# A two-direction state-space mixer: GpSimd's difference behind a VectorE shift, row scaling ahead of a logarithm, and the last unit's pieces in another order

## The chip, the cores and the metric

The kernel runs on one core of a Trainium2 chip. The core has five engines, each with its own in-order queue of instructions: TensorE (PE; its weight loads are shown as PEld), VectorE (DVE), ScalarE (ACT), GpSimd (POOL) and SyncE (SP), which here issues nearly all DMA transfers. Engines wait for each other through semaphores. The metric is the time of one execution in microseconds (us). Before the change the median of three runs is 1452.74 us (1451.16 to 1455.33).

## The reference

The input is x of shape 8 x 32 x 32 x 128 (8 sequences of 1024 tokens with 128 channels), all float32. Three stages follow each other, each added to a residual.

```python
x = x + conv_attention(group_norm(x))          # 4 heads, full attention per sequence
t = to_tokens(x)                               # (8, 1024, 128)
t = t + mixer_fwd(ln(t)) + reverse(mixer_bwd(reverse(ln(t))))
t = t + spectral_filter(ln(t))                 # 16 filters and 3 taps, one of 4 banks chosen
```

One direction of the mixer does, per sequence:

```python
z, xbc, dt = split(x @ in_proj)
xbc = silu(causal_conv4(xbc))                  # 4 taps along the tokens
xh, B, C = split(xbc)                          # 4 heads of 64 channels; state of 64
dt = softplus(dt + dt_bias); A = -exp(A_log)
# in chunks of 64 tokens: within a chunk exp of differences of cumulated dt*A,
# between chunks a state that decays and is passed on
y  = ssd(xh, dt, A, B, C) + xh * D
yg = y * silu(z)
out = (yg * rsqrt(mean(yg * yg) + eps) * norm_w) @ out_proj
```

## The kernel before

Everything that fits stays in SBUF: X holds the 8 sequences as tiles of 128 tokens x 8 x 128 channels. There are four stages in time: attention (0 to some 465 us), the mixer (465 to 1046), the transforms of the spectral filter (1046 to 1135), and its products and way back (1135 to the end). The order of instructions is written out by hand: inside each stage the program text is the order of each engine's queue (`manual_schedule`), in the mixer also SP's.

The mixer works in 16 units, one per sequence b and direction d (d = 0 forward, d = 1 backward), in the order (0,0), (0,1), (1,0) and so on. The loop body (from L1263) treats unit `u`, prepares `following` (its projections and convolution) and finishes `last` (its output projection). The pieces that matter here:

- `from_row` (L908) on GpSimd: the difference between a row of cumulated decays and a column of them, 128 x 2048 elements, read from SBUF and written in place into `lm`. By a dependency added by hand (`behind`) it waits for one more instruction, so that it runs beside the passing of states. In the loop that instruction is `following.convolved`, the second tap of the following unit's convolution on VectorE (L964). `between` (L918) on ScalarE then clips `lm` (Relu) and later takes its exponential.
- `normalize` and `normalized` prepare the layer norm of a later sequence. `normalize` takes statistics on VectorE (L446, L448) and the power -1/2 on GpSimd (L130, L132, tile `ln_r`). `normalized` then makes the shift -mean * rstd on VectorE (L453, 128 x 8, two SBUF inputs) and applies scale and shift on ScalarE (L458), eight pieces of 128 x 128, in two halves with a `yield` between them. In the loop only backward units call `normalized`.
- `chunk_states` (L1066) on TensorE makes one state per chunk in two PSUM tiles `pst`; `pass_states` on VectorE runs one copy (L1082) and 28 steps (L1085), each reading the state before it from SBUF and `pst` from PSUM. After steps 7 and 14 SP sends the states to the other half of the partitions (`moved`, L1098).
- `project_bc` (L986, tile `pb`) on TensorE follows the chunk states. `outputs(u, 0)` and `outputs(u, 1)` (L1133, tile `sy`) follow it; each is 120 to 128 small matmuls. Their PSUM tiles come from the pool `ps_s` of two buffers, the same ones as `pst`, so they also wait until the states are passed. `turn_x` (L1015, L1018) then starts the next unit.
- `end` runs the output projection of a unit (L1164, tile `spo`), sums of squares (L1176), their turning (L1190, `rms_v` L1192 on VectorE), and the power -1/2 on GpSimd (L1194, `rms`). `scale_rows` (L1202) multiplies the projected rows on ScalarE, reading PSUM; `add_rows` (L1206) adds them to X on VectorE.
- `steps` computes softplus for a fresh sequence, as a generator that is resumed by `next(going)`: matmuls (L491), small VectorE operations, Exp (L505), then u + 1 on VectorE (L508) and the logarithm on ScalarE (L510, with a table load), and last small VectorE operations (L512 to L517). Forward units with a sequence to come run it.

The last unit (7,1) stands outside of the loop. Beside its own work it finishes unit (7,0) and starts the next stage for sequence 0: `turn_spectra` (L528), `block_spectra` as generator `spectra(k)` (matmuls L539 into `pf`, a copy L547 on ScalarE; then L550 on VectorE and L554, L557 on GpSimd), `regress` (L569, tile `pu`), `add_taps` (L579) and `store_residual`. PSUM has 8 banks: `ps_w` (two buffers of two banks) and `ps_s` (the same) in the mixer; `ps_f`, `ps_t` and `ps_o` in the stage after it.

Of the kernel before, what the change touches and what calls it, by code (L numbers as in the profile page):

```python
# [8 lines left out]
F32 = mybir.dt.float32  # L9
# [5 lines left out]
P = 128  # L15
# [15 lines left out]
NB = 2  # L31
# [14 lines left out]
def fast_kernel(ctx: ExitStack, tc: tile.TileContext, a: dict, out: bass.AP, bad: bass.AP):  # L46
# [395 lines left out]
    def normalize(pool, b):  # L442
# [5 lines left out]
            nc.vector.bn_aggr(mv[:, j, :], st[:, j, :])  # L448
        return mv, rsqrt(pool, mv[:, :, 1], NT, 1.0, 1e-5, "ln_r")

    def normalized(b, pool, mv, rstd, wide=None):
        shift = pool.tile([P, NT], F32, tag="ln_s", name=f"b_shift{b}")
        nc.vector.scalar_tensor_tensor(shift, mv[:, :, 0], -1.0, rstd, ALU.mult, ALU.mult)  # L453
        xn = xns[b] = (wide or resid).tile([P, NT, C], F32, tag="ln_x", name=f"ln_x{b}")
        for j in range(NT):
            if j == NT // 2:
                yield
            nc.scalar.activation(  # L458
                xn[:, j, :], X[b][:, j, :], AF.Identity, bias=shift[:, j : j + 1], scale=rstd[:, j : j + 1]
            )  # L460
# [361 lines left out]
    with ExitStack() as s:  # L822
# [18 lines left out]
        def wide_psum(pool, name):  # L841

            return pool.tile([P, 1024], F32, tag="w", name=name)
# [60 lines left out]
        def from_row(u, other):  # L904

            t = nc.gpsimd.tensor_tensor(  # L908
                u.lm, u.cs.unsqueeze(3).to_broadcast([P, NH, NT, L]), u.lm, ALU.subtract
            )  # L910
            if other:
                behind(t, other, "beside the states")
# [158 lines left out]
                            stop=True,  # L1071
                        )

        def pass_states(u, among=range(2 * NT - 1)):

            if 0 in among:
                u.state = p1.tile([P, 2 * NT - 1, 2, HP], F32, tag="state", name=f"state{u.tag}")
                u.moved = p1.tile([P, NT, 2, HP], F32, tag="moved", name=f"moved{u.tag}")
            for k in among:
                j, c = u.chunks[k]  # L1080
                if k == 0:
                    nc.vector.tensor_copy(u.state[:, 0], u.pst[c][:, j])  # L1082
                else:
                    for h in range(2):
                        nc.vector.scalar_tensor_tensor(  # L1085
                            u.state[:, k, h, :],
                            u.state[:, k - 1, h, :],
                            u.dec[:, c, h, j : j + 1],
                            u.pst[c][:, j, h, :],
                            ALU.mult,  # L1090
                            ALU.add,
                        )
                if k in (7, 14):
                    for r in range(2):

                        ks = [m for m in range(0 if k == 7 else 8, k + 1) if u.chunks[m + 1][1] != r]
                        to = slice((1 - r) * L, (2 - r) * L)
                        nc.sync.dma_start(  # L1098
                            u.moved[to, ks[0] // 2 : ks[-1] // 2 + 1],
                            u.state[r * L : (r + 1) * L, ks[0] : ks[-1] + 1 : 2],  # L1100
                        )
# [96 lines left out]
        def scale_rows(u):  # L1198

            u.rows = u.y[:, 0, :].rearrange("p (j c) -> p j c", j=NT)  # L1200
            for j in range(NT):
                nc.scalar.activation(u.rows[:, j, :], u.po[:, j, :], AF.Identity, scale=u.rstd[:, j : j + 1])  # L1202
# [60 lines left out]
        for at, u in enumerate(units[:-1]):  # L1263
# [34 lines left out]
            next(going, None)  # L1298
            next(going, None)
            first_tap(following, 0)  # L1300
            next(going, None)
            if last:
                scale_rows(last)

            b = (u.b + 2) % B
            norm = None
# [5 lines left out]
                project_z(u, n)  # L1312
                activate_z(u, n)
            first_tap(following, 1)
            from_row(following, following.convolved)
            for _ in normalized(b, bridge, *norm) if u.d else ():
                pass
            between(following, AF.Relu, 1.0)
            chunk_states(u)
            pass_states(u)  # L1320
# [35 lines left out]
        gate(last, 1)  # L1356
        ut = tokens.tile([P, T + 2 * pad], F32, tag="xt", name="ut0")[:, : T + 4].rearrange("p (r t) -> p r t", r=4)
        copy_turned(ut, pt)
        pass_states(u, range(8))
        end(last, ps_w)  # L1360
        pass_states(u, range(8, 2 * NT - 1))
        scale_rows(last)
        sp = p2.tile([P, 2, T], F32, tag="xs", name="sp0").rearrange(
            "p a (c k i q f) -> p (a c) k i q f", k=NB, i=2, q=4, f=FC
# [15 lines left out]
            pass  # L1380
        reload(stored)
        outputs(u, 0)
        outputs(u, 1)
        making = spectra(1, "ec")
        next(making)
        add_x(u, "xdd")
        gate(u, 0)
        gate(u, 1)
        po = wide_psum(ps_w, "pu0").rearrange("p (k r c) -> p k r c", k=NB, r=4)
        for k in range(NB):  # L1390
            regress(0, k, ut, po[:, k])
        norming = normalized(1, bridge, *norm)
        next(norming)
        for _ in making:
            pass
        store_spectra(0, sp)
        end(u, ps_s)
        for _ in norming:
            pass
        for k in range(NB):  # L1400
            add_taps(0, k, po[:, k])
        store_residual(0)
# [10 lines left out]
    with ExitStack() as s:  # L1413
# [4 lines left out]
        with ExitStack() as s2:  # L1418
            p1 = s2.enter_context(tc.tile_pool(name="f_1", bufs=1))
            p2 = s2.enter_context(tc.tile_pool(name="f_2", bufs=2))  # L1420
            ps_f = s2.enter_context(tc.tile_pool(name="f_ps_f", bufs=2, space=PSUM))
            ps_t = s2.enter_context(tc.tile_pool(name="f_ps_t", bufs=1, space=PSUM))
            ps_o = s2.enter_context(tc.tile_pool(name="f_ps_o", bufs=2, space=PSUM))

            def turned(n):
# [1012 lines left out]
```

## Time and profile before

| | |
|---|---|
| median of 3 runs | 1452.74 us (1451.16 to 1455.33) |
| the profiled execution | 1452.17 us |
| its span, first to last instruction | 1450.4 us |
| TensorE busy | 1341.4 us (92%) |
| VectorE busy | 1119.2 us (77%) |
| ScalarE busy | 915.4 us (63%) |
| GpSimd busy | 528.1 us (36%) |
| DMA, mean | 85 GB/s |
| granted TensorE clock, mean | 0.980 |

Times in the views are in us from the start of the span, those of groups in ns. `out<-in` are the program's names of tiles. A wait is put down to the instruction that ended it; "issue" means that no such instruction is seen. L numbers are lines of the kernel; where a helper makes the instruction, the line is the helper's.

### The profile page before, as it was taken

What the parts mean: (1) busy time and instruction counts of PE and PEld (TensorE: products, weight loads), DVE (VectorE), ACT (ScalarE), POOL (GpSimd) and SP (SyncE); (2) the same over time, 40 slices, a digit from 0 to 9 for tenths busy, and PEclk for the clock granted to TensorE, in tenths of its full rate; (3) what the DMA queues carried; (4) which work ended last, traced back from release to release, by engine and by line L of the source; (5) the groups of instructions that cost most, each with busy time, mean ns of one, the idle gap of its engine ahead of it and who ended that gap; (6) DMA issues with size and microseconds to landing.
All of it is one profiled execution on the core that took longest, in us unless ns stands there. A gap on an engine that the chain in (4) does not pass through costs nothing. (4 is left out here: it accounts for less than half of the span.)

```text
span 1450.4 us, 45285 instructions
## 1 busy us (share of the span) xinstructions
PE 1341.4 (92%) x19782; PEld 842.2 (58%) x19782; DVE 1119.2 (77%) x2138; ACT 915.4 (63%) x1421; POOL 528.1 (36%) x510
## 2 busy tenths in 40 slices
PE   5999999999998899999989999999789899999977
PEld 2223333233333566666666666666679899999963
DVE  5779889688768598989898989898554677777745
ACT  2666666666756677778777777776344455555520
POOL 3327866875500332334342323233377111111100
PEclk9999999999999999999999999999989999999989
DMA  7101111110002333434333444442368323222258
GB/s 178 41 1 30 45 38 37 37 52 23 8 1 47 82 79 75 103 75 103 89 90 89 91 93 108 96 98 48 99 200 223 97 70 91 73 76 69 72 149 320
DMA packets 139382, 123.09 MB, mean 85 GB/s; under 512 B 44808, under 2 KB 118152, under 8 KB 135080
## 3 DMA queue, kind: packets, MB, share of 16 engines
q1 hardware_dynamic: 137064, 115.93, 31.1%
q10 hardware_dynamic: 2112, 4.19, 0.8%
q8 instruction: 157, 2.57, 0.7%
q14 instruction: 49, 0.40, 0.1%
HBM read 78.15 MB, written 34.08 MB: 77 GB/s over the span
## 5 line engine op out<-in xcount | busy, mean ns | idle before, releaser
L692 ACT ACTIVATE pr<-pt 128x1024 f32<-128x1024 f32 x256 | 248.1, 1021 | 117.2 <-PE pt L687 115.7
L717 DVE TENSOR_TENSOR two<-pr,pr 128x1024 f32<-128x1024 f32 x128 | 163.4, 1317 | 21.4 <-ACT pr L692 20.5
L1512 ACT COPY gs<-pg 128x512 f32<-128x512 f32 x256 | 132.7, 602 | 64.2 <-PE pg L1499 47.8
L1510 DVE COPY gs<-pg 128x512 f32<-128x512 f32 x256 | 158.7, 682 | 15.1 <-PE pg L1499 9.7
L687 PE MATMUL pt<-q,k 32*128 32x512 f32 x1024 | 160.1, 653 | 7.0 <-ACT pr L692 4.7
L1499 PE MATMUL pg<-taps,mst 32*128 32x128 f32 x4096 | 145.9, 282 | 4.7 <-ACT gs L1512 3.8
L1499 PEld LDWEIGHTS pg<-taps,mst 32*128 32x128 f32 x4096 | 134.1, 190 | 16.7 <-issue 11.4
L922 POOL TENSOR_TENSOR ec<-ec,ct 128x2048 f32<-128x2048 f32 x16 | 83.4, 5212 | 163.9 <-ACT cums L864 143.0
L708 PE MATMUL po<-pr,v 128*32 128x512 f32 x1024 | 141.7, 609 | 0.0
L1533 PE MATMUL py<-gs,u 128*32 128x128 f32 (+1 forms) x4096 | 128.2, 277 | 0.2 <-DVE gs L1510 0.2
L964 DVE SCALAR_TENSOR_TENSOR xs<-xp,cw,xs 128x1024 f32<-128x1024 f32 x96 | 121.8, 1282 | 3.5 <-issue 1.7
L986 PE MATMUL pb<-bxt,wbc 128*128 128x512 f32 x256 | 115.7, 605 | 8.6 <-ACT zs L977 6.0
L1533 PEld LDWEIGHTS py<-gs,u 128*32 128x32 f32 (+1 forms) x4096 | 112.2, 141 | 7.7 <-DVE gs L1510 0.4
L1522 POOL TENSOR_SCALAR u<-u 128x512 f32<-128x512 f32 x16 | 23.9, 1497 | 229.2 <-PE pg L1499 157.6
L687 PEld LDWEIGHTS pt<-q,k 32*128 32x128 f32 x1024 | 47.3, 186 | 86.2 <-issue 30.3
L1085 DVE SCALAR_TENSOR_TENSOR state<-state,dec,pst 128x64 f32<-128x64 f32 x448 | 87.4, 274 | 1.1
L986 PEld LDWEIGHTS pb<-bxt,wbc 128*128 128x128 f32 x256 | 47.7, 192 | 67.1 <-issue 54.9
L1133 PE MATMUL sy<-lm,xdt 64*64 64x64 f32 x2048 | 68.3, 224 | 17.5 <-DVE state L1085 10.5
L1194 POOL TENSOR_TENSOR rms<-rms_v,mhalf 128x8 f32<-128x8 f32 x16 | 26.2, 1636 | 151.3 <-DVE rms_v L1192 151.3
L708 PEld LDWEIGHTS po<-pr,v 128*32 128x32 f32 x1024 | 27.7, 110 | 89.5 <-issue 85.3
L1133 PEld LDWEIGHTS sy<-lm,xdt 64*64 64x64 f32 x2048 | 61.3, 136 | 30.8 <-issue 28.1
L908 POOL TENSOR_TENSOR lm<-cs,lm 128x2048 f32<-128x2048 f32 x16 | 57.9, 3617 | 46.6 <-DVE xs L964 19.5
(280 smaller groups left out, 2808.3 us busy)
## 6 DMA issues: line engine op xcount, KB each, us to landing
lm<-cd SPq DMA_DIRECT2D x32, 512.0 KB
ec<-cd SPq DMA_DIRECT2D x32, 512.0 KB
ud<-sp SPq DMA_DIRECT2D x8, 1024.0 KB
u<-ud SPq DMA_DIRECT2D x32, 256.0 KB
yd<-sums SPq DMA_DIRECT2D x32, 256.0 KB
moved<-state SPq DMA_DIRECT2D x48, 128.0 KB
yt<-yd SPq DMA_DIRECT2D x6, 1024.0 KB
X<-in_x SPq DMA_DIRECT2D x8, 512.0 KB
```

The lines of the kernel that those rows point to most:

```text
L687: nc.tensor.matmul(pt[:, i, :], lhsT=k[rows, j * P : (j + 1) * P], rhs=q[rows, cols], start=True, stop=True)
L692: nc.scalar.activation(pr[:, 2 * g : 2 * g + 2, :].rearrange("p i t -> p (i t)"), pt.rearrange("p i t -> p (i t)"), AF.Exp, scale=SCALE,)
L708: nc.tensor.matmul(po[rows, :], lhsT=vs[b][:, j, rows], rhs=pr[:, h, :], start=(j == 0), stop=(j == NT - 1))
L717: nc.vector.tensor_tensor(two, sums["pr"][:, 2 * g : 2 * g + 2, :], pr[:, 2 * g : 2 * g + 2, :], ALU.add)
L964: u.convolved = nc.vector.scalar_tensor_tensor(acc, xp[:, at : at + T], cw[u.d][:, n, i : i + 1], acc, ALU.mult, ALU.add)
L986: nc.tensor.matmul(u.pb[:, i * 512 : (i + 1) * 512], lhsT=wbc[u.d][:, k, :], rhs=xt[:, at : at + 512], start=(k == 0), stop=(k == KC - 1),)
L1085: nc.vector.scalar_tensor_tensor(u.state[:, k, h, :], u.state[:, k - 1, h, :], u.dec[:, c, h, j : j + 1], u.pst[c][:, j, h, :], ALU.mult, ...
L1133: nc.tensor.matmul(u.py[c][h * HP : (h + 1) * HP, r, j, :], lhsT=left, rhs=right, start=(kind == 0), stop=(kind == 1 or k is None),)
L1499: nc.tensor.matmul(pts[g][:, e, :], lhsT=mst[rows, n * 4 + e, :], rhs=taps[rows, cols].rearrange("p f q m i -> p (f q m i)"), start=True, ...
L1510: nc.vector.tensor_copy(to, frm)
L1512: nc.scalar.copy(to, frm)
L1533: nc.tensor.matmul(py[t * 32 : t * 32 + 32 - 16 * m, q // 2, :], lhsT=u[:, i, m:, :, :, q * FC + f].rearrange("p k b i -> p (k b i)"), rhs ...
```

## The change

There are four edits.

1. In the loop, `from_row(following, ...)` stands behind `normalized` in the program text, and in backward units it waits for that normalization's shift (kept in the list `shifted`) in place of the convolution's second tap. Forward units wait as before.
2. `scale_rows(last)` stands ahead of the resumption of `steps` that issues u + 1 and the logarithm.
3. In the last unit the states are passed in one go, ahead of `end(last)`; the second block's spectra start between the two halves of the outputs; one half of `regress` and the first half of `normalized` come ahead of `add_x` and the gates; the second half of `normalized` comes ahead of `end(u)`, and the second half of `regress` behind it.
4. In the stage after the mixer, the PSUM pool `ps_t` is opened ahead of `ps_f` and so takes the first two banks.

```diff
+    shifted = []
+
     def normalized(b, pool, mv, rstd, wide=None):
         shift = pool.tile([P, NT], F32, tag="ln_s", name=f"b_shift{b}")
-        nc.vector.scalar_tensor_tensor(shift, mv[:, :, 0], -1.0, rstd, ALU.mult, ALU.mult)
+        shifted.append(
+            nc.vector.scalar_tensor_tensor(shift, mv[:, :, 0], -1.0, rstd, ALU.mult, ALU.mult)
+        )
...
-        def pass_states(u, among=range(2 * NT - 1)):
-
-            if 0 in among:
-                u.state = p1.tile([P, 2 * NT - 1, 2, HP], F32, tag="state", name=f"state{u.tag}")
-                u.moved = p1.tile([P, NT, 2, HP], F32, tag="moved", name=f"moved{u.tag}")
-            for k in among:
-                j, c = u.chunks[k]
+        def pass_states(u):
+
+            u.state = p1.tile([P, 2 * NT - 1, 2, HP], F32, tag="state", name=f"state{u.tag}")
+            u.moved = p1.tile([P, NT, 2, HP], F32, tag="moved", name=f"moved{u.tag}")
+            for k, (j, c) in enumerate(u.chunks[:-1]):
...
             first_tap(following, 0)
-            next(going, None)
             if last:
                 scale_rows(last)
+            next(going, None)
...
             first_tap(following, 1)
-            from_row(following, following.convolved)
             for _ in normalized(b, bridge, *norm) if u.d else ():
                 pass
+            from_row(following, shifted[-1] if u.d else following.convolved)
             between(following, AF.Relu, 1.0)
...
-        pass_states(u, range(8))
+        pass_states(u)
         end(last, ps_w)
-        pass_states(u, range(8, 2 * NT - 1))
         scale_rows(last)
...
         outputs(u, 0)
-        outputs(u, 1)
         making = spectra(1, "ec")
         next(making)
+        outputs(u, 1)
+        po = wide_psum(ps_w, "pu0").rearrange("p (k r c) -> p k r c", k=NB, r=4)
+        regress(0, 0, ut, po[:, 0])
+        norming = normalized(1, bridge, *norm)
+        next(norming)
         add_x(u, "xdd")
         gate(u, 0)
         gate(u, 1)
-        po = wide_psum(ps_w, "pu0").rearrange("p (k r c) -> p k r c", k=NB, r=4)
-        for k in range(NB):
-            regress(0, k, ut, po[:, k])
-        norming = normalized(1, bridge, *norm)
-        next(norming)
+        for _ in norming:
+            pass
         for _ in making:
             pass
         store_spectra(0, sp)
         end(u, ps_s)
-        for _ in norming:
-            pass
+        regress(0, 1, ut, po[:, 1])
         for k in range(NB):
             add_taps(0, k, po[:, k])
...
+            ps_t = s2.enter_context(tc.tile_pool(name="f_ps_t", bufs=1, space=PSUM))
             ps_f = s2.enter_context(tc.tile_pool(name="f_ps_f", bufs=2, space=PSUM))
-            ps_t = s2.enter_context(tc.tile_pool(name="f_ps_t", bufs=1, space=PSUM))
             ps_o = s2.enter_context(tc.tile_pool(name="f_ps_o", bufs=2, space=PSUM))
```

## The prediction

> **What bounds the kernel now.** I read the busy table by stretch first, then the waits of the stretch that the diff touches, then single tiles and the order of time. Between 465 and 1010 us (the mixer's loop over units) TensorE is busy 503.9 of 545.0 us, VectorE 468.0, ScalarE 415.4, GpSimd 194.5: TensorE paces it, and a gain there must close a TensorE gap. The chain that ended last reaches back only to 1044 us, so it says nothing of the loop. The waits in the loop (who waited, for what, us in total, times, longest):
>
> ```profile
> PE sy L1133 <- DVE state L1085: 10.5, 7, 1.5
> PE pst L1066 <- ACT y L1202: 2.8, 6, 0.7
> PE sy L1133 <- issue: 4.7, 5, 1.5
> ACT ln_x L458 <- DVE b_shift L453: 8.3, 7, 1.2
> ```
>
> Seven waits of 1.5 us are one for each backward unit (d = 1) that has a successor; six are one for each forward unit with a fresh sequence. Who is late in the first? The row of the shift's line (152 ns at least, 3577 at most), then the timeline of VectorE and of GpSimd in such a unit (start, us, engine, line, operation; in brackets the idle time before it):
>
> ```profile
> L453 DVE SCALAR_TENSOR_TENSOR b_shift<-b_mv,ln_r x16: 152/510/3577, 370.4 to 1109.9; 128x8 f32<-128x8 f32 x16
> ...
> 809.49 2.60 DVE L964 SCALAR_TENSOR_TENSOR xs<-xp,cw,xs 128x1024 f32<-128x1024 f32 x2
> 812.30 3.57 DVE L453 SCALAR_TENSOR_TENSOR b_shift<-b_mv,ln_r 128x8 f32<-128x8 f32 x1 [0.21 <-POOL ln_r L132]
> 815.80 0.28 DVE L1082 COPY state<-pst 128x128 f32<-128x128 f32 x1
> 816.11 5.46 DVE L1085 SCALAR_TENSOR_TENSOR state<-state,dec,pst 128x64 f32<-128x64 f32 x28
> ...
> 812.24 3.61 POOL L908 TENSOR_TENSOR lm<-cs,lm 128x2048 f32<-128x2048 f32 x1
> ```
>
> The difference (L908) starts 0.06 us before the shift, and the shift ends with it (815.87 and 815.85). All seven loop shifts take 3.57 us; those with GpSimd idle take 0.15 to 0.16. The state chain, ready by 812.4 (the chunk states, L1066, end at 812.38), starts 3.4 us late. Does the chain itself suffer under the difference? The last forward unit runs both together:
>
> ```profile
> 986.36 0.29 DVE L1082 COPY state<-pst 128x128 f32<-128x128 f32 x1 [0.28 <-PE pst L1066]
> 986.76 5.46 DVE L1085 SCALAR_TENSOR_TENSOR state<-state,dec,pst 128x64 f32<-128x64 f32 x28
> ...
> 986.23 3.62 POOL L908 TENSOR_TENSOR lm<-cs,lm 128x2048 f32<-128x2048 f32 x1
> ```
>
> Same 5.46 and 3.62: no. For the logarithm, ScalarE in a forward unit, and for the last unit, VectorE and TensorE:
>
> ```profile
> 844.53 1.28 ACT L510 ACT_TABLE_LOAD   x1
> 845.82 0.26 ACT L510 ACTIVATE sp_l<-sp_u 128x64 f32<-128x64 f32 x1
> 845.98 2.16 ACT L1202 ACTIVATE y<-spo,rms 128x128 f32<-128x128 f32 x8
> 848.16 1.28 ACT L977 ACT_TABLE_LOAD   x1
> ...
> 1019.38 2.35 DVE L1107 TENSOR_TENSOR lm<-lm,bg 128x1024 f32<-128x1024 f32 x2
> 1029.20 2.72 DVE L1147 SCALAR_TENSOR_TENSOR y<-xs,dcol,sy 128x512 f32<-128x512 f32 x4 [5.13 <-PE sy L1133]
> 1045.01 1.22 DVE L1206 TENSOR_TENSOR X<-X,y 128x1024 f32<-128x1024 f32 x1 [2.65 <-ACT y L1202]
> ...
> 1031.13 5.52 PE L569 MATMUL pu<-m_u,ut 128*128 128x128 f32 x48
> 1036.49 1.95 PE L1164 MATMUL spo<-wo,y 128*128 128x128 f32 x16
> ```
>
> **What the skill says.** The Trainium skill, "SBUF — State Buffer", section "Who interferes with whom", says that a VectorE instruction with two SBUF inputs contends with a GpSimd instruction that reads SBUF, that who comes first holds the pair for the whole instruction, and that one with at most one SBUF input doesn't contend. The trace agrees on all three: the shift reads two SBUF tiles and is blocked 3.57 us; the state step reads one tile of PSUM and isn't. "ScalarE: Activation LUTs", section "What ACT_TABLE_LOAD costs", has 1283 ns a load; the trace shows 1.28 us. "TensorE: Matmul & The Clock Gate", section "HAM oscillation — how this bites in real kernels", warns of half clock after idle times of about 3.4 us; here the clock was halved at 1026.0, after a 3.0 us stall of TensorE, and matmuls of L1133 took 0.31 instead of 0.22 us.
>
> **Part 1, the difference behind the shift** (seven backward units; it replaces one VectorE instruction by another as what GpSimd waits for, no instruction is added). Before-times of the unit above: ln_r ends 812.27, the shift now takes 0.15 and ends near 812.5, the difference runs 812.5 to 816.15 (0.3 later than before), the state copy starts at 812.5 and the chain ends at 812.5 + 0.28 + 5.46 = 818.25 instead of 821.56. Queued behind the waiting difference on GpSimd is only the next product L922, 10 us later. ScalarE: ln_x starts when first_tap ends (814.7 instead of 815.91), the Relu of lm ends at 819.7 instead of 820.98. TensorE finishes pb (L986) at 819.95 as before and now finds the states done, their PSUM free and the first `moved` transfer landed (issued 3.3 us earlier, about 815.6, and 3.4 us in flight: 819.0). So the outputs follow at once. What is late next is then what is late in a forward unit, where the outputs already follow pb without a gap. From the end of pb to the first xdt of the next unit (L1018), the seven backward units need 9.42, 9.14, 9.13, 10.05, 9.13, 9.28 and 9.24 us, 65.4 in sum; forward units 6.63 in five of the six with b from 1 to 6. The check that ScalarE doesn't take over: xs 819.6 to 820.7, bt and ct to 823.4, cums and dsum to 823.9, second xs to 824.9, needed at 825.3. VectorE: four taps to 823.3, add_rows to 824.5, xdt wanted at 826.5. Gain 65.4 - 7 x 6.63 = 19.0 us. It is more than 7 x 1.5 because the backward outputs also take 2.6 and 2.4 us where forward ones take 2.1 and 2.1: they run into transfers still under way (the `moved` halves, the 512 KB reload of X) and stalls for instructions (the "issue" row), all issued behind the late states. Bounds: 10.5 (the named wait alone) and 21 (the stalls in the forward units go too).
>
> **Part 2, rows ahead of the logarithm** (six units; the same instructions and the same two table loads). rms is ready at 844.18, first_tap ends at 844.51: the rows run 844.4 to 846.6 instead of 845.98 to 848.14, the logarithm ends at 848.15 and zs starts at 849.45 as before. The logarithm's readers come after the states (855.8). TensorE's chunk states lose their 0.41 us wait and an inner stall (2.0 instead of 2.8 us), but pb still waits for zs (850.5), so TensorE gains nothing there. The state chain, xs and the second silu come 0.7 us earlier, which takes a 0.2 us stall out of turn_x: 6 x 0.2 = 1.2 us. Bounds 0 and 3.
>
> **Part 3, the last unit** (before-times). All states run in one go, 1010.42 to 1016.2 instead of 1019.46; rms_v still waits for TensorE until 1016.62, so its place behind them costs nothing. The second `moved` pair and the reload behind it on SP leave 3 us earlier. weigh_decays runs 1016.7 to 1019.05; the power on GpSimd reads SBUF beside it and may end at 1019.2 instead of 1018.5, hidden, since add_rows ends at 1022.65 as before. The outputs start when pf0_0 ends, 1019.1 instead of 1020.65, take 2.1, then pf0_1 2.0: 1023.1. Before, the second half stalled 3.0 us, from 1023.1 to 1026.1, for instructions (their 16 KB packet came at 1023.7, behind those of the reload; 256 instructions after the packet before put its due time near 1021.5, so 4.6 us passed). Now they fall due near 1019.95, come at 1024.55, and TensorE needs them at 1023.4: I keep 1.1 us of stall, and the outputs end at 1026.2 instead of 1029.25. Then add_x 2.75, both gates 2.35: 1031.4. One regress (2.8) and the earlier pf0_1 cover TensorE until 1029; it idles 2.4 us. Output projection to row scaling took 1036.49 to 1044.98, 8.5 us: now 1031.45 to 1039.95. The second regress ends at 1039.3, its add_taps at 1040.1, and add_rows (L1206) ends at 1041.35 instead of 1046.24: gain 4.9. Moved besides: ln_x and its shift go ahead of add_x and the squares, into idle time of ScalarE and VectorE (uncovered 1.6; the shift may wait 0.7 for GpSimd's sp, also idle time). sp of the second block runs on GpSimd from 1032.1 to 1035.2, just ahead of the last power (1035.9); 0.7 is the margin. On SP the stores keep their order: spectra, residual, X. The next stage's start hangs on add_rows (its statistics follow on VectorE at once), so it shifts whole. Bounds: 0 (the stall stays 3.0 and half clock follows) and 7.
>
> **Part 4, PSUM pools swapped.** ps_t takes the banks of pf0_1 instead of those of spo, so cpt no longer waits for the row scaling (3.4 us at 1045.04). But VectorE's statistics gate that stage's first pass (1046.42 to 1050.7), not cpt: 0, at most 2 if that cover goes.
>
> **Sum** against the profiled execution (1452.17 us, span 1450.4): 19.0 + 1.2 + 4.9 = 25.1, span 1425.3. The runs' median, 1452.74, is 0.6 above that execution: 1427.6.
>
> **Rivals.** (a) Only the named wait goes and the transfers and instruction stalls stay: 7 x 1.5 + 1.2 + 4.9 = 16.6, 1436. For it: the stalls called "issue" have no releaser; against: forward units, with no reload beside their outputs, hardly show them. (b) The last unit gains nothing, as TensorE now idles before its projection and may drop to half clock: 20.2, 1432.5. For it the half clock at 1026.0; against, the idle time I work out is 2.4 us. (c) More goes: part 1 at 21, part 3 at 7, 2 at the stage's start: 31, 1421.5. (d) Slower: the reload of X, now issued at 819.6, moves its 512 KB under the first half of the outputs and starves TensorE of instructions in each backward unit. One such stall was 3.0 us (1026.1); the kernel gets slower only from (25.1 + 4.4) / 7 = 4.2 us each; at 4.6, the whole delay seen in that stall, it would be 1452.74 - 25.1 + 32.2 = 1459.8. Against it: the largest stall in the loop is 1.5. (e) The swap of waits does nothing because the shift is slow by itself: excluded by its 0.15 us elsewhere.
>
> **Chances.** Forecast 0.60, (a) 0.13, (b) 0.12, (c) 0.10, (d) 0.03, and 0.02 for a stall of (d) that just eats the gain. Two runs of this kernel differ by up to 0.3% (4.4 us). The range reaches over forecast, (a), (b) and (c): 1420 to 1437; with their own spread of some 4 us each, about 0.15 of the whole falls outside. The forecast's own range is 1424 to 1431. Faster 0.95, same 0.02, slower 0.03.
>
> **What would show it.** Right: loop shifts of 0.15 to 0.2 us, L908 starting just behind them, no wait of sy on the state chain, pb to xdt about 6.6 in every unit; L1202 ahead of the load for L510; the outputs of the last unit at 1019 less the shift, add_rows 5 us nearer to them. Wrong: "issue" waits at L1133 of over 1 us in several units, a second half-clock window near the last projection, or a state step longer than 195 ns beside L908.

## The result, and the profile after

The changed kernel takes 1431.35 us (median, 1427.85 to 1434.45), the kernel before 1454.03 us beside it (1451.16 to 1456.32): a ratio of 0.9846, with a 95% interval of 0.9821 to 0.9871, so about 22 us less. The forecast was 1427.6 with a range of 1420 to 1437. The profiled execution of the changed kernel took 1432.01 us, its span is 1430.2 us (before: 1452.17 and 1450.4). Its lines have moved by a few: the shift is L456, the difference L912, pb L990, zs L981, the states L1084 and L1087, sy L1135, rows L1204.

I cut both spans at the first xdt of the loop, at the last unit's xdt, at the end of the last add_rows and at the end of the last pu:

| stretch | before, us | after, us | gain |
|---|---|---|---|
| up to the loop's first xdt | 483.1 | 483.6 | -0.5 |
| loop, first xdt to the last unit's | 517.0 | 502.3 | 14.7 |
| last unit, to the end of add_rows | 46.2 | 41.05 | 5.1 |
| next stage, to the last pu | 82.9 | 82.8 | 0.1 |
| products and way back | 321.3 | 320.5 | 0.8 |

The waits of the changed kernel between 465 and 1010 us (who waited, for what, us in total, times, longest):

```profile
PE pb L990 <- ACT zs L981: 11.3, 15, 1.5
...
PE sy L1135 <- issue: 5.8, 9, 1.2
```

The wait of sy for the states, 10.5 us before, is gone. Two things have grown instead: pb's wait for zs, the silu of z on ScalarE (6.0 us before), and sy's "issue" stalls (4.7 before). The shift in all its runs (shortest, median and longest, ns):

```profile
L456 DVE SCALAR_TENSOR_TENSOR b_shift<-b_mv,ln_r x16: 153/168/605, 368.7 to 1090.6; 128x8 f32<-128x8 f32 x16
```

The seven of the loop take 0.166 to 0.168 us, where they took 3.57. The order of time in a backward unit (VectorE, then GpSimd, start and us), the same unit that the prediction showed:

```profile
804.30 0.17 DVE L456 SCALAR_TENSOR_TENSOR b_shift<-b_mv,ln_r 128x8 f32<-128x8 f32 x1 [0.21 <-POOL ln_r L132]
804.51 0.29 DVE L1084 COPY state<-pst 128x128 f32<-128x128 f32 x1
804.83 5.46 DVE L1087 SCALAR_TENSOR_TENSOR state<-state,dec,pst 128x64 f32<-128x64 f32 x28
810.21 5.12 DVE L968 SCALAR_TENSOR_TENSOR xs<-xp,cw,xs 128x1024 f32<-128x1024 f32 x4
...
804.60 3.63 POOL L912 TENSOR_TENSOR lm<-cs,lm 128x2048 f32<-128x2048 f32 x1 [0.33 <-DVE b_shift L456]
```

The difference starts 0.13 us behind the end of the shift, and the states run beside it at their old pace, 0.21 us after the shift's start instead of 3.50. ScalarE in a forward unit, and VectorE and TensorE in the last unit:

```profile
833.68 2.16 ACT L1204 ACTIVATE y<-spo,rms 128x128 f32<-128x128 f32 x8
835.85 1.28 ACT L514 ACT_TABLE_LOAD   x1
837.15 0.26 ACT L514 ACTIVATE sp_l<-sp_u 128x64 f32<-128x64 f32 x1
837.42 1.28 ACT L981 ACT_TABLE_LOAD   x1
838.72 1.94 ACT L981 ACTIVATE zs<-pz 128x1024 f32<-128x1024 f32 x2
...
1011.60 2.72 DVE L1149 SCALAR_TENSOR_TENSOR y<-xs,dcol,sy 128x512 f32<-128x512 f32 x4 [1.41 <-PE sy L1135]
1024.39 1.41 DVE L583 SCALAR_TENSOR_TENSOR X<-pu,keep,X 128x512 f32<-128x512 f32 x2 [3.31 <-PE pu L573]
1025.72 1.22 DVE L1208 TENSOR_TENSOR X<-X,y 128x1024 f32<-128x1024 f32 x1
...
1015.60 0.46 PE L1166 MATMUL spo<-wo,y 128*128 128x128 f32 x2 [1.17 <-DVE y L1160]
1021.51 2.84 PE L573 MATMUL pu<-m_u,ut 128*128 128x128 f32 x24
```

The rows stand ahead of the logarithm now, but both table loads still stand between them and zs. In the last unit VectorE's wait for the outputs shrank from 5.13 us to 1.41, and what add_rows comes behind is no longer the row scaling (it waited 2.65 us for it) but add_taps, behind the second regress.

The figure that the prediction stood on, from the end of pb to the next xdt, in the seven backward units: before 9.42, 9.14, 9.13, 10.05, 9.13, 9.28, 9.24 (65.4 in sum), after 6.59, 7.45, 7.35, 7.06, 6.39, 7.64, 7.86 (50.3). The forecast was 7 x 6.63 = 46.4. Five of the seven contain an "issue" stall of sy: 0.74, 0.73, 0.35, 0.93 and 1.24 us, 4.0 in sum, about the 3.9 by which the forecast was missed. (The view of the waits counts nine: three more are small ones of forward units, and one of 1.1 us stands in the last forward unit, (7,0), beside whose outputs no reload runs; the kernel before has it too, 1.09 us. The last unit, (7,1), has none any more.) In the units that stall, a 16 KB packet of instructions starts within 0.25 us of the end of the reload's 2 KB packets: in the one at 612 the reload moves until 609.8, the instruction packet starts at 609.81, and sy, in want of instructions from 611.4, resumes at 612.16. In the unit without a stall (804 to 818) the packet came at 811.77, ahead of the reload's, which begin at 812.5.

### The profile page after: what moved, and what is told of

It reads as the page before. It is cut to its first block, busy times and chain, and to the rows that moved or that the text cites. A ratio compares the mean times of both kernels' runs of the same rounds, so it can differ in the third digit from the quotient of the medians.

```text
span 1430.2 us, 45285 instructions
## 1 busy us (share of the span) xinstructions
PE 1334.7 (93%) x19782; PEld 839.8 (59%) x19782; DVE 1095.4 (77%) x2138; ACT 914.5 (64%) x1421; POOL 529.5 (37%) x510
## 5 line engine op out<-in xcount | busy, mean ns | idle before, releaser
L1500 PEld LDWEIGHTS pg<-taps,mst 32*128 32x128 f32 x4096 | 134.0, 189 | 17.1 <-issue 11.6
L990 PE MATMUL pb<-bxt,wbc 128*128 128x512 f32 x256 | 116.9, 610 | 13.9 <-ACT zs L981 11.3
L990 PEld LDWEIGHTS pb<-bxt,wbc 128*128 128x128 f32 x256 | 48.2, 193 | 73.1 <-issue 55.6
L1087 DVE SCALAR_TENSOR_TENSOR state<-state,dec,pst 128x64 f32<-128x64 f32 x448 | 87.3, 274 | 1.1
L912 POOL TENSOR_TENSOR lm<-cs,lm 128x2048 f32<-128x2048 f32 x16 | 57.9, 3621 | 50.2 <-DVE xs L968 33.8
L732 PE MATMUL pd<-two,ones 128*32 128x512 f32 x512 | 73.0, 613 | 0.2
L1166 PEld LDWEIGHTS spo<-wo,y 128*128 128x128 f32 x512 | 62.1, 191 | 15.3 <-issue 10.3
```

Of the source, the lines that this page charges most:

```text
L990: nc.tensor.matmul(u.pb[:, i * 512 : (i + 1) * 512], lhsT=wbc[u.d][:, k, :], rhs=xt[:, at : at + 512], start=(k == 0), stop=(k == KC - 1),)
L1087: nc.vector.scalar_tensor_tensor(u.state[:, k, h, :], u.state[:, k - 1, h, :], u.dec[:, c, h, j : j + 1], u.pst[c][:, j, h, :], ALU.mult, ...
L1500: nc.tensor.matmul(pts[g][:, e, :], lhsT=mst[rows, n * 4 + e, :], rhs=taps[rows, cols].rearrange("p f q m i -> p (f q m i)"), start=True, ...
```

## The experiments

The first four kernels make one part of the change each. The kernel before took 1456.19 us beside them.

**Part 1 alone.**

```diff
-        nc.vector.scalar_tensor_tensor(shift, ...)
+        shifted.append(nc.vector.scalar_tensor_tensor(shift, ...))
...
-            from_row(following, following.convolved)
             for _ in normalized(b, bridge, *norm) if u.d else ():
                 pass
+            from_row(following, shifted[-1] if u.d else following.convolved)
```

> Part 1 alone in the kernel before. Theory (the shift, which reads two SBUF tiles, was held by the running difference, and the states and outputs behind it came late): the seven loop shifts take 0.15 to 0.2 us, no output waits for the states, and the sum from the end of pb to the next xdt over the seven backward units falls from 65.4 to about 50 us as in the whole change; 14 to 16 us less than before. Rival (the parts help each other, and the gain needs the earlier row scaling too): under 10 us less.

1439.09 us, ratio 0.9887 (0.9845 to 0.9929), 17.1 us less. The loop is 502.55 us, as in the whole change, and the backward units need 50.3 us from pb to xdt, again as there. So part 1 makes the loop's gain by itself, and it falls short of 19.0 by itself: nothing of the shortfall comes from the other parts.

**Part 2 alone.**

```diff
+            if last:
+                scale_rows(last)
             next(going, None)
-            if last:
-                scale_rows(last)
```

> Part 2 alone in the kernel before. Forecast of the prediction: 1.2 us less. What the trace of the change suggests: the chunk states of six forward units end 0.8 us earlier, but pb still starts only after zs and TensorE fills the rest with stalls for instructions, so 0, between 1 less and 1 more.

1454.09 us, ratio 0.9985 (0.9971 to 0.9999). The timed runs leave room for 2 us; the profile shows no place for them: the loop is 517.08 us, where that of the kernel before is 516.96. The waits of TensorE between 465 and 1010 us:

```profile
PE pb L986 <- ACT zs L977: 11.3, 15, 1.5
```

Before, pst waited 2.8 us for the rows and pb 6.0 for zs. Now the first wait is gone and the second has grown by 5.3 (the stalls inside the chunk states have joined it): TensorE waits one step later for the same ScalarE.

**Part 3 alone** (the last unit's order, with the pools as before).

```diff
-        pass_states(u, range(8))
+        pass_states(u)
         end(last, ps_w)
-        pass_states(u, range(8, 2 * NT - 1))
...
         outputs(u, 0)
-        outputs(u, 1)
         making = spectra(1, "ec")
         next(making)
+        outputs(u, 1)
...
+        regress(0, 0, ut, po[:, 0])
...
         end(u, ps_s)
+        regress(0, 1, ut, po[:, 1])
```

> Part 3 alone in the kernel before, with the PSUM pools in the old order. If part 4 is worth nothing, the whole 5 us of the last unit come here: add_rows of the last unit ends 41 us after the first xdt of that unit, where the kernel before has 46.2. If the swapped pools are needed for it, 2 us or less.

1452.37 us, ratio 0.9976 (0.9961 to 0.9992). In the profile the last unit takes 41.03 us instead of 46.16, the same 5.1 as in the whole change. But those 46.16 us hold a stall of 3.0 us, at whose end the clock was halved for 3.4 us. The kernels with part 1 alone and with part 4 alone run the last unit in the old order too; they take 43.33 and 43.11 us for it, with a stall of 1.6 and 1.4 us and no half clock under the outputs. TensorE's stall for instructions in the last unit, in the kernel before and in that with part 4 alone:

```profile
PE sy L1133 <- issue: 3.0, 1, 3.0
...
PE sy L1133 <- issue: 1.4, 1, 1.4
```

So the new order is worth 2.1 to 5.1 us in profiles, depending on the one that it is held against; the interval of the timed runs is 1.2 to 5.7 us. The loop, whose text is that of before, took 520.6 us in this profile instead of 517.0, with "issue" stalls of sy of 5.9 us instead of 4.7 and 3.4 us at half clock from 756.6.

**Part 4 alone.**

```diff
+            ps_t = s2.enter_context(tc.tile_pool(name="f_ps_t", bufs=1, space=PSUM))
             ps_f = s2.enter_context(tc.tile_pool(name="f_ps_f", bufs=2, space=PSUM))
-            ps_t = s2.enter_context(tc.tile_pool(name="f_ps_t", bufs=1, space=PSUM))
```

> Part 4 alone in the kernel before. Forecast of the prediction: cpt of the next stage (L528) no longer waits 3.4 us for the row scaling, but the statistics on VectorE gate that stage, so nothing within what a run can tell. From the last add_rows to the last pu matmul the kernel before has 82.9 us; the same within 0.5. Rival: up to 2 us less there.

One execution, 1456.19 us. The next stage takes 83.06 us (before 82.91), so nothing was gained. Why, TensorE's order of time around its start shows:

```profile
1045.71 1.06 PE L528 MATMUL cpt<-ident,ln_x 128*128 128x128 f32 x8 [0.87 <-DVE X L579]
1048.23 3.72 PE L539 MATMUL pf<-fwd,ln_x 128*128 128x256 f32 x16 [1.46 <-ACT y L1202]
```

cpt waits for add_taps (L579) instead of the row scaling, from which I take it that ps_t has the banks of pu0; and the matmuls after it, whose pool now has the row scaling's banks, wait for that. The wait changes its owner. (The loop took 524.6 us here, untouched by this edit, with 6.9 us of "issue" stalls and twice 6.8 us at half clock. The untouched loop's own spread, 517 to 525 us, is why every loop figure below is read from its units and waits, not from its length alone. The units have a spread too: the seven backward ones need 65.4 us from pb to xdt in the profile before, 68.0 in that of part 3 alone and 72.1 here. Against these part 1 gains 15 to 22 us, and the forecast was made against the low end.)

The next four go together: the change once more, and three kernels made from it. The kernel before took 1453.9 us beside them.

**The change again.**

> The whole change, repeated as the yardstick of the three kernels beside it: 0.984 to 0.986 of the kernel before, about 22 us less. If the stalls named issue at L1135 come from where packets of instructions happen to fall against the reload of X, they appear again in four to six of the seven backward units, 3 to 5 us in sum between 465 and 1000 us, perhaps in other units than in the first profile.

1433.49 us, ratio 0.9841 (0.9811 to 0.9871), loop 502.35 us, last unit 41.04 us. The backward units stall for instructions 0.81, 1.02, 0.64, 0.78 and 1.28 us, 4.5 in sum, in the same five units as in the first profile: not a chance of one execution.

**The reload of X later.** It is issued behind the decays of the next unit, in the last unit behind the store of the spectra.

```diff
-            if stored:
-                reload(stored)
-            stored = None
+            waiting, stored = stored, None
...
             take_decays(following)
+            if waiting:
+                reload(waiting)
+            waiting = None
```

> The change, with the 512 KB reload of X issued behind the next unit's decays (in the last unit behind the store of the spectra), so that it no longer runs while the outputs do. Theory: the reload delays TensorE's packets of instructions, and that is the 4 us by which part 1 fell short of its forecast: the issue stalls at L1135 fall from about 4.0 us in the backward units and 1.1 us in the last unit to under 0.5 in all, from the end of pb to xdt the backward units take 6.4 each as the forward units do, and the kernel is 3 to 5 us faster than the change (1426 to 1428 where that is 1431). Rival 1: TensorE uses up 256 instructions [...]faster than any packet comes, with or without other traffic: the stalls stay, within 1 us of the change. Rival 2: the reload only meets another packet, later, and the stall moves to the next unit's matmuls: L1135 clean, time within 1 us of the change.

1431.53 us, ratio 0.9835 (0.9807 to 0.9863). Its waits of TensorE between 465 and 1000 us, where the change has 5.8 us, 9 times, for sy:

```profile
PE sy L1135 <- issue: 1.9, 5, 1.0
```

In the backward units the stalls fall from 4.0 us to 0.4, and from pb to xdt these units take 46.6 us, against the 46.4 of the forecast. The loop is 498.4 us, 3.9 less than the change's. So the reload is what delayed the instructions there. The theory fails in two places: the small stalls of forward units stay (0.31, 0.17 and 0.12 us), and so do the 1.05 us that I had called the last unit's. They belong to unit (7,0), beside whose outputs no reload runs: every profile on record has this stall, 1.0 to 1.4 us, and these runs don't name its cause. And no gain can be seen in the timed runs. Of the 3.9 us, 1.6 are lost in the last unit, 42.61 us instead of 41.05, and 2.6 in the way back (52.7 instead of 50.1 us), whose text is the same and for which I have no cause. The 1.6 us have one. The last unit around the start of its output projection, in the change and then in this kernel (stretch and its length; busy time of TensorE, its loads, VectorE, ScalarE, GpSimd; granted clock; DMA share and GB/s):

```profile
1013.19:1016.60 3.41, 1.70 (x14) 1.35 (x12) 3.41 (x5) 1.06 (x1) 0.00 (x0) 1.00 0.00 0
1016.60:1020.01 3.41, 3.37 (x35) 2.67 (x36) 1.19 (x2) 2.97 (x6) 2.74 (x6) 1.00 0.02 5
...
1010.84:1014.25 3.41, 1.66 (x13) 1.31 (x12) 3.41 (x5) 1.63 (x2) 0.00 (x0) 1.00 0.00 0
1014.25:1017.66 3.41, 3.41 (x24) 2.63 (x26) 0.59 (x1) 2.02 (x5) 3.07 (x6) 0.50 0.00 0
```

Here the clock was halved for 3.41 us under the projection: fourteen matmuls of spo take 2.88 us instead of 1.83, the sums of squares 1.61 instead of 1.07, together 1.6. That the later reload brought this about is not shown: the stretch ahead of it hardly differs, and the last section comes back to it.

**Four more VectorE instructions with two SBUF inputs** between the shift and the states. They compute a product that nobody reads.

```diff
             from_row(following, shifted[-1] if u.d else following.convolved)
+            if u.d:
+                junk = bridge.tile([P, NT], F32, tag="junk_s", name=f"junk{u.tag}")
+                for _ in range(4):
+                    nc.vector.scalar_tensor_tensor(junk, norm[0][:, :, 0], -1.0, norm[1], ALU.mult, ALU.mult)
```

> The change, and in each backward unit four more VectorE instructions of the shift's size (128x8, two SBUF inputs, a result nobody reads) behind the difference in program order, so between the shift and the states. Theory (one pair of ports, whole instructions, first come first served): one of the four is held until the difference L912 ends, about 3.5 us, the other three take 0.15 each; the states are about 4 us later than in the change, sy waits 1.5 to 2 us for L1087 again, and 13 to 17 us of the gain are lost: 1444 to 1449. If the four get ahead of the difference instead, all take 0.15, the difference starts 0.6 us later, and the time is that of the change. Rival: the 3.57 us were not the ports but the wait for ln_r: none takes more than 0.2, no loss.

1458.83 us, ratio 1.0028 (1.0012 to 1.0044): 0.3% slower than the kernel before. VectorE and GpSimd in a backward unit:

```profile
820.01 0.17 DVE L456 SCALAR_TENSOR_TENSOR b_shift<-b_mv,ln_r 128x8 f32<-128x8 f32 x1 [0.21 <-POOL ln_r L132]
820.10 4.07 DVE L1323 SCALAR_TENSOR_TENSOR junk<-b_mv,ln_r 128x8 f32<-128x8 f32 x4
824.21 0.29 DVE L1084 COPY state<-pst 128x128 f32<-128x128 f32 x1
...
820.32 3.63 POOL L912 TENSOR_TENSOR lm<-cs,lm 128x2048 f32<-128x2048 f32 x1 [0.33 <-DVE junk L1323]
```

The four take 0.16, 0.17, 3.48 and 0.17 us, in this unit and within 0.01 us in the other six. The first two start before the difference does, the third is held to its end, the fourth is free again. The theory of the ports stands. Its price was mis-sized: the loss is 25 us, not 13 to 17. I had counted sy's wait for the states alone (15.5 us, as forecast). Most of what was missing is shown by the kernel before with a later reload, further down. The rest goes with the clock: in five of the seven units it was halved for 3.4 or 6.8 us, and these take 10.45 to 11.97 us from pb to xdt, the two at full clock 9.85 and 9.89.

**Four more with one input in PSUM.**

```diff
-                    nc.vector.scalar_tensor_tensor(junk, norm[0][:, :, 0], -1.0, norm[1], ALU.mult, ALU.mult)
+                    nc.vector.scalar_tensor_tensor(junk, norm[0][:, :, 0], -1.0, u.pz[:, :NT], ALU.mult, ALU.mult)
```

> As the kernel with four more instructions of two SBUF inputs, but their second input lies in PSUM. Theory: none is held beside the difference L912, 0.15 to 0.2 us each, 0.8 us in all, for which the state chain has 1.6 us of room: the time of the change within 1.5 us. Rival: any VectorE instruction is held beside that difference: one takes 3.5 us and the loss is the same 13 to 17 us.

1440.35 us, ratio 0.9906 (0.9873 to 0.9939), about 7 us over the change. VectorE and GpSimd in the same unit:

```profile
808.01 0.75 DVE L1323 SCALAR_TENSOR_TENSOR junk<-b_mv,pz 128x8 f32<-128x8 f32 x4 [1.17 <-ACT zs L981]
808.80 0.29 DVE L1084 COPY state<-pst 128x128 f32<-128x128 f32 x1
...
806.97 3.62 POOL L912 TENSOR_TENSOR lm<-cs,lm 128x2048 f32<-128x2048 f32 x1 [0.33 <-DVE b_shift L456]
```

All four run in the middle of the difference and take 0.16 us each: not one is held, in none of the seven units. That settles the question of the ports. The expected time was missed for another reason, which I had not seen: the tile they read is also read by zs on ScalarE, and the first of the four waits 1.17 us for that. With their own 0.75 us the states come 1.9 us later, and these units take 56.9 us from pb to xdt instead of 50.3: the room of 1.6 us that I had given the state chain was not there.

**The kernel before, with the reload later.** The same edit as above, made to the kernel before (1453.54 us beside it).

> The kernel before, with the reload of X issued behind the next unit's decays, as in the kernel with the change and a later reload. It parts the gain of part 1 into the named wait and the collisions. Theory (the prediction's): of the 9.34 us from the end of pb to the first xdt in a backward unit, 6.4 are work, 1.5 the wait for the states, and the rest, about 1.4, is outputs that run into the reload and into packets of instructions held up by it: it falls to 7.9 to 8.2, 8 to 10 us less in the seven, 1444 to 1447 where the kernel before is 1454. Rival: the rest comes from the late states themselves (their `moved` halves in flight, the instructions behind them): 9.1 to 9.4 stay, within 2 us of before.

1450.07 us, ratio 0.9985 (0.9966 to 1.0004). From pb to xdt: 9.18, 9.13, 9.13, 9.12, 9.13, 9.13 and 9.13 us, 63.95 instead of 65.4. The timed runs differ from the kernel before by no more than their interval. So only 1.5 us of the 65.4 were collisions with the reload (the profiles with 68.0 and 72.1 us lie 4.1 and 8.1 over it, half clock included), and 9.13 is a floor that something else sets. VectorE, ScalarE and TensorE in such a unit (its pb ends at 813.71):

```profile
809.87 5.46 DVE L1085 SCALAR_TENSOR_TENSOR state<-state,dec,pst 128x64 f32<-128x64 f32 x28
815.25 5.11 DVE L964 SCALAR_TENSOR_TENSOR xs<-xp,cw,xs 128x1024 f32<-128x1024 f32 x4
822.84 2.35 DVE L1018 TENSOR_TENSOR xdt<-sx,dt 128x1024 f32<-128x1024 f32 x2 [1.35 <-PE sx L1015]
...
820.71 1.06 ACT L969 ACTIVATE xs<-xs 128x1024 f32<-128x1024 f32 x1
...
821.82 1.42 PE L1015 MATMUL sx<-ident,xs 128*128 128x128 f32 x11 [0.29 <-ACT xs L969]
```

The states are followed on VectorE by four taps, the taps by the silu on ScalarE, the silu by sx, and sx by xdt: VectorE's own queue behind the late states, with no transfer in it. The kernel with four held instructions agrees: its states start 4.20 us after the shift's start instead of 3.50, and the shortest of its backward units takes 9.85 instead of 9.13. That is 0.70 and 0.72. In the change the states start 3.29 us earlier than before and the floor falls by 2.74, to 6.39; the other 0.55 I put down to TensorE's own work, which then ends last. The lost 2.74 us a unit, 19.2 in seven, is what part 1 gave back, and what the held instructions took away again.

**The logarithm later.** The change with the logarithm behind the Relu of the next unit's differences.

```diff
                 scale_rows(last)
-            next(going, None)
...
             between(following, AF.Relu, 1.0)
+            next(going, None)
             chunk_states(u)
```

> The change, with the logarithm of part 2 moved again: behind the Relu of the next unit's differences, ahead of the chunk states (no table load is taken away, one is added). It asks why part 2 gave nothing. Theory: in the change TensorE has its chunk states done 1.2 us before ScalarE's zs, since two table loads (2.56 us) and the logarithm stand between the rows and zs; with the logarithm later, zs starts about 1.3 us earlier, the wait of pb for zs falls from 11.3 to about 4 us between 465 and 1000 us, and the logarithm with its loads fits into the 2.95 us in which ScalarE waits for the taps. Six forward units gain 0.9 to 1.2 each: 5.4 to 7.2 us under the change, about 1425. Rival: the logarithm's readers on VectorE, or ScalarE's xs behind the added load, become late instead and turn_x waits: within 1.5 us of the change.

1428.72 us, ratio 0.985 (0.9823 to 0.9876), loop 497.5 us, 4.8 less than the change's. TensorE's waits between 465 and 1000 us:

```profile
PE sy L1135 <- issue: 4.4, 5, 1.3
PE pb L990 <- ACT zs L981: 3.6, 8, 0.5
PE sx L1019 <- ACT xs L973: 3.3, 7, 0.6
```

Both theories are half right. pb's wait for zs falls by 7.7 us, as expected; 3.0 of that comes back as sx waiting for xs, the rival. A forward unit has no stall of its own any more, and its period is 34.57 us against 34.99 at best in the change: it now hangs on VectorE's queue (states, logarithm's readers, taps), which starts 0.03 us behind the chunk states and has no room left. In the timed runs this gain can't be told from none: the change's ratios are 0.9846 and 0.9841.

**Both later.** The logarithm as above, and the loop's reload later; the last unit's reload stays.

> The change with both: the logarithm later and, in the loop only, the reload of X later (the last unit's stays where the change has it). If the two are independent, the loop from the first xdt to the last unit's is 9 to 11 us shorter than the change's 502.3, and the kernel takes 1420 to 1423. If the half clock of TensorE falls on the last unit's projection, as in the kernel with the later reload, 1.6 us are lost there; if the reload meets the logarithm's unit in some new place, less than 8 us are gained.

1423.7 us (1420.84 to 1429.15), ratio 0.9818 (0.979 to 0.9847), loop 494.75 us. That is 7.5 us less than the change's loop, not 9 to 11: one stall for instructions, 0.87 us, has appeared in a forward unit that had none so long in the change, and the logarithm gave less than its forecast. Since the gain over the change is about what single runs differ by, I ran it again:

> The kernel with the logarithm and the loop's reload later, once more, since its gain over the change (5 to 8 us) is about what two rounds of one kernel differ by. If the gain is real: median 1420 to 1427, below the change's 1431.4 and 1433.5; loop from the first xdt to the last unit's 493 to 497 us. If the first result was chance: median 1429 or more.

1427.57 us (1423.86 to 1429.49), ratio 0.9816 (0.9798 to 0.9834), loop 496.05 us. Its backward units stall for 1.6 us in sum, where the first profile had none, and the last unit met the half clock (42.0 us instead of 40.4). The median lies just over the band named for a real gain and under that for chance; the ratio to the kernel before is the same as the first time, and the middle of all eleven times is 1426.3, that of the change's ten is 1432.5. This is the fastest version, some 6 us under the change, though the intervals of their ratios overlap.

## Why the prediction was right, and where it was not

| step | forecast, us | measured in the profile, us |
|---|---|---|
| 1, difference behind the shift | 19.0 | 15.1 |
| 2, rows ahead of the logarithm | 1.2 | none that the profile shows (-0.2) |
| 3, last unit | 4.9 | 5.1 (2.1 against the profile of part 4 alone) |
| 4, pools | 0 | 0.1 |
| sum, of the span | 25.1 | 20.3 (the small rest lies in units and stretches not touched) |

**Part 1, the mechanism: right, and shown.** The shift was held by the difference, and the states don't suffer beside it. The Trainium skill, "SBUF — State Buffer", section "Who interferes with whom", says so of instructions with two SBUF inputs and of those with one; the pair of experiments agrees with both halves (3.48 us against 0.16, in seven units each).

**Part 1, the size: the term that was mis-sized is the 7 x 6.63.** The work itself is even less than that, 6.39 us. But stalls for instructions of 4.0 us came in, which I had seen in the kernel before and weighed too low: it is rival (d), at 0.6 us per unit where I had worked out that it turns the sign at 4.2. The step that failed is the check of what falls due at the same time: the reload was "now issued at 819.6", while the outputs use up 256 instructions in some two microseconds. The later reload, which brings the units to 46.6 us, shows the cause. The Trainium skill, "Runtime: NRT & Kernel Launch", section "Instruction fetch mechanics", calls the fetch of such 16 KiB blocks of 256 instructions mostly hidden; the size agrees with the trace (157 such packets on one queue, about 250 of TensorE's instructions for each), the hiding does not hold here, with 0.35 to 1.24 us of stall.

**Part 1, the reason for the excess over 10.5: wrong.** I said that backward units lost more than the named wait because their outputs run into transfers. The kernel before with a later reload still takes 9.13 us a unit; what held it was VectorE's queue behind the states. Collisions were the smaller part in the profile that I had read, and a larger one in two others. The 6.63 was a fair figure (6.39 to 6.59 without a stall) because I took it from the forward units, where that queue isn't late, and not from the reason.

**Part 2: one step held, its 1.2 us were not there.** The step "which takes a 0.2 us stall out of turn_x" holds: without a stall a forward unit takes 6.40 us instead of 6.63. In the change three of the six lost 0.5 to 0.6 us instead, in which small stalls for instructions (0.24, 0.30 and 0.18 us) lie. That pb goes on waiting for zs was said and is so; moving the logarithm off that path is what gains there.

**Part 3: the sum was right, several terms were not.** The outputs start at the end of pf0_0 (1004.84, pf0_0 ends at 1004.91), as said. The stall of 1.1 us that I kept didn't come: in the change no sy of the last unit waits for instructions. In its place pf0_1 waited 0.62 us for the rows behind it, a cost I had called hidden (the power beside weigh_decays took 2.60 us instead of 1.64). The projection starts 6.7 us earlier against the unit's xdt, where I had 5.0, mostly since it begins behind the first gate, where I had waited for both; it then idles 0.6 us for the second. The add_taps of both halves run behind the second regress, 1.41 us where I had 0.8, and end behind the row scaling (1025.80 against 1025.02), which takes much of that back. That 4.9 agrees with 5.1 is also luck of the profile: held against part 4 alone, whose last unit has the old order, it is 2.1. The 3.0 us of stall in the profile before, which I took for a property of the kernel, were 1.4 and 1.6 in two others.

**Part 4: right in its zero, wrong in its reason.** By the waits the banks came from pu0, not from pf0_1, and the wait passed on to add_taps.

**The rivals.** The median lies 0.4 us outside the forecast's own range of 1424 to 1431, and nearest to it in time is (b), 1432.5, which is not what happened in the change: the loop fell short, the last unit did not. The half clock of (b) did come in other kernels of the same last unit, at 1.6 us.

## What to carry to other kernels

When one instruction is blocked, price its removal from a unit of the same kernel in which it isn't blocked, and follow the blocked engine's own queue to the next thing that another engine waits for; the named wait (10.5 us here) was little more than half of what the late states cost. Then ask which bulk transfer now moves under the densest stretch of small instructions: here a 512 KB reload cost 4 us of the 19 until it was issued elsewhere. Before a stall is counted as a saving, see whether other profiles of the same text have it: one of 3.0 us was 1.4 in the next. Moving a piece of work that doesn't end the wait only moves the wait (rows, PSUM pools); look for what stands between the released engine and the next thing that it is waited for, here two table loads.

## What the runs showed of the hardware that I had not expected

- A block of instructions is delayed by a bulk transfer of the same core: with the reload beside the outputs, TensorE's stalls in the seven backward units come to 3.0 to 4.5 us in sum in the five profiles whose states aren't late; with the reload elsewhere they are 0.4, 0 and 1.6 us in three. The stall of 1.0 to 1.4 us in unit (7,0) doesn't go with it, and its cause stays open.
- The half clock isn't decided by the length of one idle time. Before the last projection and in it TensorE idled 1.17 and 0.58 us in the change, at full clock, and 1.16 and 0.59 us in the kernel with the later reload, where the clock was halved. The Trainium skill, "TensorE: Matmul & The Clock Gate", section "HAM oscillation — how this bites in real kernels", names idle times of over 3.4 us; none here is as long. The traces suggest what decides: all changes of the clock in a trace lie on one grid of 3.41 us (within 0.002 us), and what counts seems to be how much idle time falls into one step of it. In the nine kernels with the new last unit, the four that lost the clock here had 1.71 to 1.75 us in one step, the five that kept it 1.11 to 1.71. So where the grid happens to fall would decide, not the edit. No run set this, and it is no sharp rule: in the loop of the kernel with four held instructions a step with 1.82 us kept the clock.
- An instruction of 0.17 us that starts 0.2 us after GpSimd's difference has begun takes 3.48 us; the two just ahead of it took 0.16 and 0.17.
